# Four convolution layers on 4 x 384 x 64 x 64: the last layer's first input loaded during the mixer, its stores issued by GpSimd, its maxima taken by pieces, and layer 1's taps handed over per band

## The chip, the cores and the metric

The kernel runs on one core of a Trainium2 chip. The core has a matrix engine (TensorE, PE in the profile; PEld is its weight load), VectorE (DVE), ScalarE (ACT), GpSimd (POOL) and SyncE (SP, which only issues DMAs). Every engine works through its own list of instructions in order and waits on semaphores; a DMA that an engine issues also has its place in that list. The metric is the device time of one execution in microseconds; less is better. Everything is float32.

## The reference

The input is 4 batches of 384 channels by 64 x 64 points. Four layers follow one another, each added to its input: `x = x + layer(_gn(x))`, where `_gn` normalizes each batch over 32 groups of 12 channels.

- Layer 0: attention over the 4096 points on the first 96 channels, then a 384 x 384 projection of all channels.
- Layer 1: a 384 x 384 product, a filter in the Fourier domain of each 8 x 8 tile, a depthwise 3 x 3 convolution (nine taps per channel), `gelu(x1) * x2` of the two halves of the channels, and a 192 to 384 product.
- Layer 2: depthwise 3 x 3 and 5 x 5 convolutions joined by gates to a "token" map, batch norms over all batches, and a mixer: 384 to 768, GELU, 768 to 384, batch norm. The result is gated against the layer's input.
- Layer 3, per batch and channel, cut to what matters here:

```python
x_avg = x.mean(axis=(2, 3)); x_max = x.max(axis=(2, 3))
x_w  = gelu(x_avg @ w_avg.T + b_avg + x_max @ w_max.T + b_max)
xr   = (x_w[:, :, None] * w_mix[None, :, :]).reshape(b, c, 7, 7)
Gx   = sqrt(sum(xr * xr, axis=(2, 3)));  Nx = Gx / (Gx.mean(axis=1) + EPS)
kern = gamma * (xr * Nx) + beta
out  = depthwise 7x7 convolution of x with kern, one kernel per batch and channel
```

The layer sees `_gn(x)`, so the 7 x 7 kernels of a batch are known only when that batch's mean, variance and maximum per channel are known, over all three groups of 128 channels. And layer 2's last batch norm needs the mixer's output of all four batches before any batch of layer 3 can start.

## The kernel before, in words

The 384 channels are three groups `j` of 128 partitions. The Python program emits instructions batch by batch; a scheduler then sets the order on each engine, with the place in the program as its priority, and pools of buffers decide when a tile's memory comes free for the next.

**Layers 0 and 1** (`phase_a`, 0 to about 2426 us). Attention of batch b is emitted side by side with layer 1 of batch b − 1 (`layer1`, L787 to L823). Layer 1 goes by tiles of 8 rows and 16 columns: `h` counts the eight bands of 8 rows, `w` the four tiles in a band. When a band and its neighbours are there, `band_taps` (L897 to L930) makes the depthwise convolution: for each channel group nine taps, nearly all on VectorE (L918), then the GELU and the product of the halves. It is a generator: with each `next` it hands over one channel group, at the tiles w = 1, 2, 3 of a later band. `band_out` (L932 to L942) makes the last product and stores. In the last batch (`alone`), where no attention runs beside it, some taps go to TensorE instead.

**Layer 2** (`phase_b`, then `phase_ef`, L1274). After the convolutions come two loops. The first (E, 3250 to 3764 us) makes the 384 to 768 product and stores it (`hidden`, stored from ACT's queue, L1372). It also makes `wx`, the part of the result that does not pass the mixer, and stores it from GpSimd's queue (L1371). The second (F, the mixer, 3772 to 4268 us) loads blocks of `hidden` of 128 x 6 x 1024 (L1385, 3 MB each), applies the GELU (L1387), multiplies (L1397), copies out (L1404), takes statistics (L1405), and stores `h2` in blocks of 128 x 3 x 1024 from GpSimd's queue (L1407). The last batch's `h2` stays on the chip (`h2_last`). The pools of E and F are opened together and closed together.

**Layer 3** (`phase_g`, L1428) takes the batches in the order 3, 0, 1, 2.

- `x2_of(b)` (L1555 to L1625) makes the input of layer 3 for a batch: for j = 1, 2, 0 it loads `wx` (2 MB, L1564, SP), and for each of four pieces of 1024 columns loads `h2` (L1570, not for batch 3), scales it on ACT into PSUM (L1574), adds it into x on VectorE (L1575) and squares on ACT with a running sum (L1577). Then VectorE takes the maximum over all 4096 columns in one instruction (L1579). For j = 1 and 2, x is stored for later (L1584, SP). After the third group come the small steps of the norm (L362 to L380), the two small products for `x_w` (L1595), its GELU (L1605) and the scales `a_s`, `a_b`, `b_s` (L1608 to L1621).
- The dense part of the 7 x 7 kernel is made from `w_mix` and a band matrix as Toeplitz tiles and run on TensorE; `to_strips` (L1627) scales x and transposes it into `z` for that. The constant part (`beta`) is a 7 x 7 box sum, made by `boxes` (L1692 to L1761): sums of rows on GpSimd (L1725, L1727) and VectorE, a transpose and a product with `cols7` on TensorE (L1748, L1754), added into x (L1756); the finished x of a batch and channel group is stored as `rest` (L1760, SP; the DRAM side has 4096 runs of 512 bytes).
- `phase_g` emits `x2_of(b)` step by step with `to_strips` and `boxes` for j = 0 of the batch before. When all four batches are through, `conv7` (L1657 to L1690) runs over j = 0, 1, 2: GpSimd makes each third Toeplitz tile and VectorE the others (L1668), TensorE multiplies (L1681), VectorE adds `rest` (L1689). Beside it `half_strips` (L1508) and `boxes` prepare j = 1 and 2; those load the stored x2.
- The x tiles are 16 KB per partition; three buffers with the tag `x` serve `x2_of` and the later boxes. A tile of j = 1, 2 is free when its store has landed, that of j = 0 only when the boxes are through and the `rest` store has landed.

Of the kernel before, what the change touches and what calls it, by code (L numbers as in the profile page):

```python
# [28 lines left out]
NJ = 3  # L29
P = 128  # L30
# [196 lines left out]
class _Builder:  # L227
# [550 lines left out]
    def layer1(self, b):  # L778

        nc = self.nc
        st = self.stats_tile("x1_st")
        norm, alone = self.norm1, b == B - 1
        if alone:
            self.tap_weights()
        xb, tt, cf, acc = {}, {}, {}, {}  # L787
        for n in range(-2, 4 * 11):
            h, w = n // 4, n % 4
            if n + 2 < 32:  # L790
                if (n + 2) % 4 == 0:
                    x = self.block("xa_in", self.xa[b], (n + 2) // 4, bufs=1)
                xb[n + 2] = self.tile_norm(x, (n + 2) % 4, norm, alone)
            if n < 0:
                continue
            if n < 32:
                tt[n] = self.tile_hidden(xb.pop(n))
            if 0 < n < 33:
                cf[n - 1] = self.tile_filter(tt.pop(n - 1))
            if 1 < n < 34:  # L800
                self.tile_back(cf.pop(n - 2), (n - 2) // 4, (n - 2) % 4)
            if n < 34:
                yield 3.75

            if w == 1 and 0 < h < 9:
                self.halo(h - 1)
            if w == 1 and 1 < h < 10:
                acc[h - 2] = []
                taps = self.band_taps(h - 2, alone, acc[h - 2])
            if w and 1 < h < 10:  # L810
                next(taps, None)
                yield 0.0
            if w == 0 and h > 2:
                k = h - 3
                yield from self.band_out(b, acc.pop(k), k, st)
        r, gm, n, mv = self.norm_of_stats(st)
        nc.vector.tensor_copy(self.r2[:, :, b], r)
        nc.vector.tensor_copy(self.n2[:, :, b], n)
        nc.vector.tensor_sub(self.p2[:, :, b], mv[:, :, 0], gm)
        nc.vector.tensor_mul(self.p2[:, :, b], self.p2[:, :, b], r)  # L820
# [450 lines left out]
        nc.vector.scalar_tensor_tensor(self.about, self.c1_u, -1.0, self.base, ALU.mult, ALU.subtract)  # L1271
        yield

    def phase_ef(self):  # L1274
        tc, nc = self.tc, self.nc
        with ExitStack() as ctx:
            self.open_psum(ctx)
            cp = ctx.enter_context(tc.tile_pool(name="e_const", bufs=1))
            io = ctx.enter_context(tc.tile_pool(name="e_io", bufs=2))
            hp = ctx.enter_context(tc.tile_pool(name="e_h", bufs=2))  # L1280
            w1 = self.weight(cp, "cm_w1_t")
            w2 = self.weight(cp, "cm_w2_t")
            cg1 = self.weight(cp, "cg_w1_t")
            cg2 = self.weight(cp, "cg_w2_t")

            a, c = self.bn_scale_shift("bn_ar", *self.over_batches("ar", self.mvt), self.vec("ar_g"), self.vec("ar_b"))
            gp = self.sm([P, NJ, B], "gp")
# [31 lines left out]
                nc.vector.tensor_mul(self.gn[:, j, :], self.n2[:, j, :], stay)  # L1319


            st = cp.tile([P, 6, B * 8, 6], F32, tag="h_st", name="h_st")
            sums = cp.tile([P, NJ, B, 4], F32, tag="wx_sum", name="wx_sum")
            for b in range(B):
                for i in range(4):
# [50 lines left out]
            a1, c1 = self.bn_scale_shift("bn_h", mv[:, :, 0], mv[:, :, 1], self.vec("cm_g1"), self.vec("cm_b1"))  # L1376


            st2 = cp.tile([P, NJ, B * 8, 6], F32, tag="h2_st", name="h2_st")
            mvb = cp.tile([P, NJ, B, 2], F32, tag="h2_mvb", name="h2_mvb")  # L1380
            for b in range(B):
                for i in range(4):
                    blk = slice(i * 1024, (i + 1) * 1024)
                    h = hp.tile([P, 6, 1024], F32, tag="h", name="f_h")
                    nc.sync.dma_start(h, self.hidden[b][:, :, blk].rearrange("o p n -> p o n"))  # L1385
                    for o in range(6):
                        nc.scalar.activation(  # L1387
                            h[:, o, :], h[:, o, :], AF.Gelu, bias=c1[:, o : o + 1], scale=a1[:, o : o + 1]
                        )
                    out = self.h2_last[:, :, blk]  # L1390
                    if b < B - 1:
                        out = io.tile([P, NJ, 1024], F32, tag="x", name="f_h2")
                    for j in range(NJ):
                        for v in range(2):
                            m = self.pm("h2_m")
                            for o in range(6):
                                nc.tensor.matmul(  # L1397
                                    m,
                                    lhsT=w2[:, o, j * P : (j + 1) * P],
                                    rhs=h[:, o, v * 512 : (v + 1) * 512],  # L1400
                                    start=o == 0,
                                    stop=o == 5,
                                )
                            nc.scalar.copy(out[:, j, v * 512 : (v + 1) * 512], m)  # L1404
                            nc.vector.bn_stats(st2[:, j, 8 * b + 2 * i + v, :], out[:, j, v * 512 : (v + 1) * 512])  # L1405
                    if b < B - 1:
                        nc.gpsimd.dma_start(self.h2[b][:, :, blk], out)  # L1407
                for j in range(NJ):
                    nc.vector.bn_aggr(mvb[:, j, b], st2[:, j, 8 * b : 8 * b + 8].rearrange("p a b -> p (a b)"))
            mv = self.sm([P, NJ, 2], "h2_mv")  # L1410
# [18 lines left out]
    def phase_g(self):  # L1429
# [8 lines left out]
        with ExitStack() as ctx:  # L1438
            self.open_psum(ctx, 3)
            cp = ctx.enter_context(tc.tile_pool(name="g_const", bufs=1))  # L1440
            self.gx_p = ctx.enter_context(tc.tile_pool(name="g_x", bufs=1))
            self.gw_p = ctx.enter_context(tc.tile_pool(name="g_w", bufs=2))
            self.gt_p = ctx.enter_context(tc.tile_pool(name="g_t", bufs=2))
            self.w_gate = []
# [63 lines left out]
    def half_strips(self, j, half):  # L1508

        nc = self.nc  # L1510
        for pair in range(2):
            for part in range(3):
                y = self.gx_p.tile([P, 11 * P], F32, tag="y", name="ax2", bufs=2)
                lo, hi = (22 * part - 1) * W, (22 * part + 21) * W
                inside = slice(max(lo, 0) - lo, min(hi, N) - lo)
                for u in range(2):
# [38 lines left out]
    def x2_of(self, b):  # L1555
# [2 lines left out]
        nc = self.nc  # L1558
        mv = self.sm([P, NJ, 2], "gn_mv")
        mx = self.sm([P, NJ], "max")  # L1560
        for j in (1, 2, 0):
            at = lambda v: v[:, j, b : b + 1]
            x = self.gx_tile("x2")
            nc.sync.dma_start(x, self.wx[b][:, j])  # L1564
            var = self.sm([P, 4], "x2_var")
            for q in range(4):
                sl = slice(q * 1024, (q + 1) * 1024)
                if b < B - 1:
# [6 lines left out]
                nc.vector.tensor_add(x[:, sl], x[:, sl], m)  # L1575

                nc.scalar.activation(h, x[:, sl], AF.Square, bias=at(self.neg2), accum_out=var[:, q : q + 1])  # L1577
                yield None
            nc.vector.tensor_reduce(mx[:, j : j + 1], x, AX.X, ALU.max)  # L1579
            nc.vector.tensor_copy(mv[:, j, 0:1], at(self.mean2))  # L1580
            nc.vector.tensor_reduce(mv[:, j, 1:2], var, AX.X, ALU.add)
            nc.vector.tensor_scalar(mv[:, j, 1:2], mv[:, j, 1:2], 1.0 / N, None, ALU.mult)
            if j:
                nc.sync.dma_start(self.scratch["x2"][b][j], x)  # L1584
        r, gm, n, _ = self.norm_of_groups(mv, True)
        avg = self.sm([P, NJ], "avg")
        nc.vector.tensor_sub(avg, mv[:, :, 0], gm)
# [38 lines left out]
    def to_strips(self, j, b, x):  # L1626
# [1 line left out]
        nc = self.nc  # L1628

        for part in range(3):  # L1630
            y = self.gx_p.tile([P, 11 * P], F32, tag="y", name="ax2", bufs=2)
            lo, hi = (22 * part - 1) * W, (22 * part + 21) * W
            if part == 0:
                nc.gpsimd.memset(y[:, 0:W], 0.0)
# [57 lines left out]
    def boxes(self, j, b, x):  # L1692
# [8 lines left out]
        for part in range(4):  # L1701
# [55 lines left out]
                if q == 0:  # L1757
                    yield
            if part == 3:
                nc.sync.dma_start(self.rest[j][:, :, b], x.rearrange("p (y n) -> p y n", n=P))  # L1760
            yield  # L1761


# [1 line left out]
def tile_conv_preact4(ctx, tc, ins, out):  # L1765
    k = _Builder(ctx, tc, ins, out)
    with ExitStack() as strips:
        k.phase_a(strips)
        k.phase_b()
        k.phase_ef()  # L1770
        k.phase_g()
    return k

# [17 lines left out]
```

## Time and profile before

| | |
|---|---|
| runs before | 5096.59, 5099.97, 5101.0 us; median 5099.97 us |
| profiled execution: its own time | 5109.2 us |
| its span | 5107.4 us |
| mean granted clock of TensorE | 0.947 |
| busy in the span: PE, PEld | 4618.5 us (90%), 2618.1 us (51%) |
| busy: DVE, ACT, POOL | 2736.5 us (54%), 2080.9 us (41%), 730.1 us (14%) |
| last matmul of the mixer ends | 4268.3 us |
| scales of batches 3, 0, 1, 2 ready (L1620) | 4352.7, 4406.9, 4501.7, 4577.4 us |
| dense convolution starts (L1681) | 4591.3 us |

The profiled execution is one of its own and was 9 us longer than the median of the runs. Times in the text are counted from the start of its span. "Busy" is the time in which an engine worked on something; a wait names the instruction whose end released the waiting one. A group of rows "x12" has twelve instructions, and its mean is that of one.

### The profile page before, as it was taken

The page shows a single profiled execution, that of the slowest core. Times are in us where ns is not written, and L with a number is a line of the kernel's source. Part 1 is how long each engine was busy: PE and PEld are TensorE (multiplying, and loading weights), DVE is VectorE, ACT ScalarE, POOL GpSimd, SP SyncE. Part 2 cuts the span into 40 slices and gives each one's busy share as a digit, 9 for nine tenths or more (in the row PEclk, how much of TensorE's full clock was granted, in tenths as well). Part 3 has the DMA queues.
Part 4 walks back from the last instruction along what each step waited for, and adds up shares of the span by engine and source line. Part 5 has one row for each costly group of instructions (what it writes and reads, how often), then busy time and mean ns, then how long its engine had stood idle before and what let it go on. Part 6 is the DMA issues. An engine that isn't in the chain of part 4 may idle for free. (4 is left out here: it accounts for less than half of the span.)

```text
span 5107.4 us, 47835 instructions
## 1 busy us (share of the span) xinstructions
PE 4618.5 (90%) x17875; PEld 2618.1 (51%) x17875; DVE 2736.5 (54%) x4432; ACT 2080.9 (41%) x2789; POOL 730.1 (14%) x524
## 2 busy tenths in 40 slices
PE   5999999989999999999988999599999995559999
PEld 2333444334443344435467888244444442448999
DVE  5322566634556445555867877554421114658775
ACT  4444344454444544445345665311133334652320
POOL 1000000000000000000035555000000000125433
PEclk9999999999999999998989999799999997569999
DMA  5210211111112101112259999766644434658776
GB/s 171 62 48 29 89 62 62 56 50 44 56 62 77 38 31 62 62 60 91 90 165 274 293 294 286 248 245 241 231 181 148 152 149 166 241 165 247 219 225 189
DMA packets 387541, 723.28 MB, mean 142 GB/s; under 512 B 21627, under 2 KB 221158, under 8 KB 380390
## 3 DMA queue, kind: packets, MB, share of 16 engines
q1 hardware_dynamic: 333528, 519.50, 32.8%
q10 hardware_dynamic: 28494, 105.99, 5.3%
q0 software_dynamic: 25280, 94.65, 4.8%
q8 instruction: 144, 2.36, 0.2%
q14 instruction: 95, 0.78, 0.0%
HBM read 432.48 MB, written 287.57 MB: 141 GB/s over the span
## 5 line engine op out<-in xcount | busy, mean ns | idle before, releaser
L733 PE MATMUL av<-probs,vt 128*128 128x512 f32 x2048 | 972.3, 612 | 0.0
L704 ACT ACTIVATE probs<-sc_s 128x1024 f32<-128x1024 f32 x512 | 498.4, 1020 | 784.1 <-PE av L733 767.6
L733 PEld LDWEIGHTS av<-probs,vt 128*128 128x128 f32 x2048 | 377.9, 195 | 482.6 <-issue 478.9
L1127 PE MATMUL conv_m<-toep,z 128*128 128x256 f32 x2304 | 521.6, 386 | 11.1 <-DVE toep L1108 6.8
L918 DVE SCALAR_TENSOR_TENSOR acc<-band,vecs,acc 128x512 f32<-128x512 f32 x708 | 507.3, 747 | 45.0 <-POOL band L879 24.0
L1397 PE MATMUL h_m<-f_h,cm_w_t 128*128 128x512 f32 x1152 | 496.2, 594 | 7.9 <-ACT f_h L1387 7.9
L1127 PEld LDWEIGHTS conv_m<-toep,z 128*128 128x128 f32 x2304 | 440.3, 193 | 72.9 <-DVE z L1060 4.9
L1348 PE MATMUL h_s<-e_tok,cm_w_t 128*128 128x512 f32 x768 | 364.5, 598 | 5.4 <-DVE e_tok L1333 5.4
L1681 PE MATMUL conv_m<-toep,z 128*128 128x128 f32 x3072 | 364.3, 277 | 1.2 <-DVE rest_o L1689 1.1
L1397 PEld LDWEIGHTS h_m<-f_h,cm_w_t 128*128 128x128 f32 x1152 | 219.4, 191 | 284.7 <-issue 273.9
L1108 POOL TENSOR_TENSOR toep<-w,band 128x1536 f32<-128x1536 f32 x94 | 323.5, 3442 | 285.9 <-PE conv_m L1127 248.1
L1681 PEld LDWEIGHTS conv_m<-toep,z 128*128 128x128 f32 x3072 | 355.3, 194 | 1.6 <-issue 1.3
L696 PE MATMUL sc_s<-q,k 32*128 32x512 f32 x2048 | 301.9, 647 | 13.0 <-ACT probs L704 10.3
L841 PE MATMUL t_m<-w_in_t,xb 128*128 128x384 f32 x768 | 277.1, 495 | 1.8 <-DVE coef L858 0.9
L766 PE MATMUL proj_m<-xm,w_proj_t 128*128 128x512 f32 x576 | 268.0, 604 | 7.3 <-DVE xm L719 7.3
L1355 ACT COPY e_h<-h_s 128x1024 f32<-128x1024 f32 x96 | 97.2, 1012 | 419.1 <-PE h_s L1348 419.1
L773 DVE SCALAR_TENSOR_TENSOR x_res<-proj_m,bn_c,x_res 128x512 f32<-128x512 f32 x96 | 71.8, 748 | 348.7 <-PE proj_m L766 345.7
L1348 PEld LDWEIGHTS h_s<-e_tok,cm_w_t 128*128 128x128 f32 x768 | 147.7, 192 | 192.3 <-issue 185.6
L1357 DVE BATCH_NORM_STATS2 h_st<-e_h 128x6 f32<-128x512 f32 x192 | 123.4, 685 | 188.7 <-ACT e_h L1355 188.6
L1405 DVE BATCH_NORM_STATS2 h_st<-f_h 128x6 f32<-128x512 f32 x72 | 50.0, 694 | 322.8 <-ACT f_h L1404 322.8
L841 PEld LDWEIGHTS t_m<-w_in_t,xb 128*128 128x128 f32 x768 | 142.1, 191 | 139.2 <-issue 61.7
L1348 PE MATMUL h_s<-z,cm_w_t 128*128 128x512 f32 x384 | 198.7, 600 | 12.5 <-DVE z L1333 12.5
(365 smaller groups left out, 6216.4 us busy)
## 6 DMA issues: line engine op xcount, KB each, us to landing
d<-d_o ACTq DMA_DIRECT2D x96, 512.0 KB
c_d<-d SPq DMA_DIRECT2D x96, 512.0 KB
hid<-e_h ACTq DMA_DIRECT2D x16, 3072.0 KB
f_h<-hid SPq DMA_DIRECT2D x16, 3072.0 KB
x_in<-in_x SPq DMA_DIRECT2D x96, 256.0 KB
x_res<-in_x SPq DMA_DIRECT2D x32, 768.0 KB
xa<-x_res POOLq DMA_DIRECT2D x32, 768.0 KB, 3.9
xa_in<-xa SPq DMA_DIRECT2D x32, 768.0 KB
```

Of the source, the lines that this page charges most:

```text
L696: nc.tensor.matmul(s[:, g], lhsT=k4[32 * g : 32 * g + 32, c], rhs=q[i][32 * g : 32 * g + 32], start=True, stop=True,)
L704: nc.scalar.activation(p[:, h * 1024 : (h + 1) * 1024], s[:, 2 * h : 2 * h + 2].rearrange("p a b -> p (a b)"), AF.Exp, scale=0.25,)
L733: nc.tensor.matmul(av, lhsT=vt[:, 4 * c + v, :], rhs=p[:, v * 512 : (v + 1) * 512], start=c == 0 and v == 0, stop=c == 7 and v == 3,)
L766: nc.tensor.matmul(m, lhsT=self.w_proj[:, j, o * P : (o + 1) * P], rhs=xm[:, j], start=j == 0, stop=j == NJ - 1,)
L841: nc.tensor.matmul(m[:, 0:C], lhsT=xb[:, j], rhs=self.w_in[:, j, :], start=j == 0, stop=j == NJ - 1,)
L918: nc.vector.scalar_tensor_tensor(out, src(j, k), w, done, ALU.mult, ALU.add)
L1108: eng.tensor_tensor(t, self.w53[:, at : at + 192].rearrange("p (m n) -> p m n", n=8).unsqueeze(2).to_broadcast([P, 24, 8, 8]), band.rearra ...
L1127: nc.tensor.matmul(m[:, c * 256 : (c + 1) * 256], lhsT=self.z_[:, at : at + P], rhs=t[:, 12 * c + 4 * i : 12 * c + 4 * i + 4].rearrange("p ...
L1348: nc.tensor.matmul(s[:, v, :], lhsT=w1[:, j, o * P : (o + 1) * P], rhs=t[j][:, v * 512 : (v + 1) * 512], start=j == 0, stop=j == NJ - 1,)
L1357: nc.vector.bn_stats(st[:, o, 8 * b + 2 * i + v, :], h[:, o, v * 512 : (v + 1) * 512])
L1397: nc.tensor.matmul(m, lhsT=w2[:, o, j * P : (j + 1) * P], rhs=h[:, o, v * 512 : (v + 1) * 512], start=o == 0, stop=o == 5,)
L1681: nc.tensor.matmul(m[:, ch * P : (ch + 1) * P], lhsT=self.z_[:, at : at + P], rhs=t[:, 8 * c + 2 * i : 8 * c + 2 * i + 2].rearrange("p m a ...
```

## The change

Five edits, in the order of the diff.

1. In `layer1`, for the first three batches, all three channel groups of a band's taps are emitted at once at tile w = 1, those of bands 6 and 7 together. In the last batch they are emitted group by group as before.
2. `phase_ef` closes E's pools (`e_const`, `e_io`) before F. In the memory that is released, on the right side, the pool of the x tiles is opened already there, with batch 3's three tiles (`x2_ahead`). Their loads from `wx` are emitted in the mixer's last batch, one at each of the blocks i = 1, 2, 3. F's output tiles are 128 x 1024, three of them, and `h2` is stored in 36 pieces instead of 12. The strips' tiles (`ax2`) move to another pool.
3. `x2_of` takes batch 3's tiles from that list and loads the others as before.
4. Its maximum is taken by pieces of 1024 columns, each behind its piece's square, and a last instruction takes the maximum of the four.
5. The stores of x2 and of `rest` are issued by GpSimd instead of SP.

```diff
-            if w == 1 and 1 < h < 10:
+            if alone and w == 1 and 1 < h < 10:
                 acc[h - 2] = []
                 taps = self.band_taps(h - 2, alone, acc[h - 2])
-            if w and 1 < h < 10:
+            if alone and w and 1 < h < 10:
                 next(taps, None)
+                yield 0.0
+            if not alone and w == 1 and 1 < h < 9:
+                for k in (6, 7) if h == 8 else (h - 2,):
+                    acc[k] = []
+                    for _ in self.band_taps(k, alone, acc[k]):
+                        pass
                 yield 0.0
...
+    x2_order = 1, 2, 0
+
-    def phase_ef(self):
+    def phase_ef(self, strips):
...
+            cp = ctx.enter_context(tc.tile_pool(name="ef_const", bufs=1))
             w2 = self.weight(cp, "cm_w2_t")
+            hp = ctx.enter_context(tc.tile_pool(name="ef_h", bufs=2))
+            first = ctx.enter_context(ExitStack())
+            ep = first.enter_context(tc.tile_pool(name="e_const", bufs=1))
+            io = first.enter_context(tc.tile_pool(name="e_io", bufs=2))
...
+            first.close()
+            self.gx_p = strips.enter_context(tc.tile_pool(name="g_x", bufs=1, side="right"))
+            self.x2_ahead = [self.gx_tile("x2") for _ in range(NJ)]
+            io = ctx.enter_context(tc.tile_pool(name="f_io", bufs=3))
...
-                    out = self.h2_last[:, :, blk]
-                    if b < B - 1:
-                        out = io.tile([P, NJ, 1024], F32, tag="x", name="f_h2")
+                    if b == B - 1 and 0 < i:
+                        j = self.x2_order[i - 1]
+                        nc.sync.dma_start(self.x2_ahead[i - 1], self.wx[b][:, j])
                     for j in range(NJ):
+                        out = self.h2_last[:, j, blk]
+                        if b < B - 1:
+                            out = io.tile([P, 1024], F32, tag="x", name="f_h2")
...
-                    if b < B - 1:
-                        nc.gpsimd.dma_start(self.h2[b][:, :, blk], out)
+                        if b < B - 1:
+                            nc.gpsimd.dma_start(self.h2[b][:, j, blk], out)
...
-            x = self.gx_tile("x2")
-            nc.sync.dma_start(x, self.wx[b][:, j])
-            var = self.sm([P, 4], "x2_var")
+            if b == B - 1:
+                x = self.x2_ahead.pop(0)
+            else:
+                x = self.gx_tile("x2")
+                nc.sync.dma_start(x, self.wx[b][:, j])
+            var, top = self.sm([P, 4], "x2_var"), self.sm([P, 4], "x2_max")
...
                 nc.scalar.activation(h, x[:, sl], AF.Square, bias=at(self.neg2), accum_out=var[:, q : q + 1])
+                nc.vector.tensor_reduce(top[:, q : q + 1], x[:, sl], AX.X, ALU.max)
                 yield None
-            nc.vector.tensor_reduce(mx[:, j : j + 1], x, AX.X, ALU.max)
+            nc.vector.tensor_reduce(mx[:, j : j + 1], top, AX.X, ALU.max)
...
             if j:
-                nc.sync.dma_start(self.scratch["x2"][b][j], x)
+                nc.gpsimd.dma_start(self.scratch["x2"][b][j], x)
...
             if part == 3:
-                nc.sync.dma_start(self.rest[j][:, :, b], x.rearrange("p (y n) -> p y n", n=P))
+                nc.gpsimd.dma_start(self.rest[j][:, :, b], x.rearrange("p (y n) -> p y n", n=P))
```

In the order of instructions that the scheduler makes of the changed program, the three loads of batch 3's x do not stand in the mixer's last batch: they stand on SP directly behind the load of the mixer's first `hidden` block and ahead of the second, and wait for the end of E. On GpSimd the `x2` and `rest` stores stand among the box sums of the next batch and, in the convolution, among the Toeplitz tiles.

## The prediction

> **What bounds the kernel now.** I read the slices first, then stage windows, then the order of time across the seam between mixer and last layer, then the waits of the last layer, then the rows of GpSimd's own DMA issues. The slices:
>
> ```profile
> PE   5999999989999999999988999599999995559999
> PEclk9999999999999999998989999799999997569999
> ```
>
> TensorE is the bound nearly everywhere; four slices are half empty, and three of them lie together near the end, where its clock drops too. The windows of the mixer, of what lies between it and the dense 7x7 convolution (I call it the head), and of that convolution (columns: stretch, length, busy of PE, PEld, DVE, ACT, POOL, clock, DMA share, GB/s):
>
> ```profile
> 3772.00:4268.30 496.30, 496.21 (x1152) 219.39 (x1152) 71.81 (x108) 161.75 (x191) 8.62 (x12) 1.00 0.36 135
> 4268.30:4591.30 323.00, 145.81 (x706) 130.43 (x705) 199.50 (x318) 192.30 (x270) 54.62 (x53) 0.58 0.61 219
> 4591.30:5107.40 516.10, 487.51 (x4196) 479.81 (x4196) 370.64 (x413) 120.70 (x206) 230.10 (x139) 0.98 0.75 220
> ```
>
> The mixer leaves PE no gap, and a third of the DMA is used: room for loads. In the head no engine is busy over 62%: a chain of dependences sets it. There the change has its place. The seam in order of time (start, length, instruction):
>
> ```profile
> 4273.92 1.21 ACT L1574 ACTIVATE x_m<-z,g,gh 128x1024 f32<-128x1024 f32 x1 [1.11 <-DVE g L1420]
> ...
> 4276.55 2.12 SPq L1564 DMA_DIRECT2D x<-wx  x3
> ...
> 4286.91 2.35 DVE L1575 TENSOR_TENSOR x<-x,x_m 128x1024 f32<-128x1024 f32 x2 [7.57 <-DMA x<-wx]
> ...
> 4293.84 1.19 ACT L1574 ACTIVATE x_m<-z,g,gh 128x1024 f32<-128x1024 f32 x1
> 4294.05 0.32 SPq L1584 DMA_DIRECT2D x<-x  x1
> 4294.06 4.42 DVE L1579 TENSOR_REDUCE max<-x 128x1 f32<-128x4096 f32 x1
> ...
> 4324.70 0.15 DVE L375 TENSOR_TENSOR gn_d<-gn_d,gn_mv 128x3 f32<-128x3 f32 x1
> ```
>
> The scaled h2 piece is there at 4275.13; the add waits for its x until 4286.91. Each channel group then ends in a reduce of 4.42 us. Three groups take 4286.91 to 4321.65, and batch 3's norm starts at 4324.70. Who waits in 4268 to 4592:
>
> ```profile
> POOL box L1725 <- DVE x L1575: 115.6, 6, 37.5
> PE gn_pv L362 <- DVE gn_d L375: 96.4, 4, 46.4
> ```
>
> TensorE waits in all four batches for statistics that end such a row of adds. In the convolution stage, the waits of POOL and PE and of SP's rest stores:
>
> ```profile
> POOL toep L1668 <- PE conv_m L1681: 141.6, 49, 7.6
> ...
> PE box_m L1754 <- ACT ht L1750: 11.4, 7, 4.5
> PE ht_m L1748 <- ACT z L1535: 10.5, 5, 3.8
> ```
> ```profile
> SPq L1760 <- DVE in_x L1756: 21.2, 8, 5.8
> ```
>
> PE loses about 23 us there, so little can be won; POOL makes each third Toeplitz tile, with 2.9 us to spare on average (141.6/49). GpSimd's DMA issues, the nearest rows to the moved stores:
>
> ```profile
> L776 POOL DMA_DIRECT2D xa<-x_res x32 | 23.1, 723 | 648.2 <-DVE x_res L773 648.2
> ...
> L637 POOL DMA_DIRECT2D shift<-zero x16 | 8.7, 554 | 0.9 <-DMA shift<-zero 0.7
> L1407 POOL DMA_DIRECT2D h<-f_h x12 | 8.6, 718 | 419.6 <-ACT f_h L1404 419.6
> ```
>
> **The change part by part.** The sum is made against the profiled execution (span 5107.4, its own time 5109.2); the median of the runs, 5099.97, is 9.2 lower, 0.18%. I take the difference off the median. About 0.2%, 10 us, is what can be told from no change.
>
> *1, batch 3's x2 loads in the mixer.* Three loads leave the seam, so the first add can follow the first scaled piece: 4286.91 − 4275.13 = **11.8 us won**. The price is at the mixer's start. In the new order the three loads (6.3 MB) stand on SP directly behind the first hidden load and ahead of the second, and their memory comes free with the last matmul of the stage before (3764.2). In the old trace the second hidden load landed at 3784.75, its Gelus ended at 3790.5, and PE needs them only after the first block (3772.09 + 30.9 = 3803.0): 12.5 us to spare. 6.3 MB at the 295 to 308 GB/s of the windows there is 21 us late; at the 400 GB/s that a full DMA share would give (135 GB/s at share 0.36 scales to 375; 308 at 0.75 to 410) 16 us late. Loss 3 to 8 us if all three go ahead whole, 0 if the queues share. I take **+3**; ends 0 and +16, if the room is not there at all.
>
> *2, maxima by pieces.* 12 reduces of 4.42 us become 48 of 128x1024 and 12 of 128x4. A piece lies between 1.10 (a quarter of 4.42) and 1.22 (the add of that shape, L1575); 128x4 is 0.15 (L1581). DVE's own work grows by 12 × (4 × 1.16 + 0.15 − 4.42) = 4 us. But the reduces now lie between adds, where DVE waited for ACT: ACT's pair of scale and square takes 2.27 us per piece (4291.58 to 4293.84), DVE's pair 1.22 + 1.16 = 2.4. A group becomes 4 × 2.4 + 0.45 small = 10.1 against 11.58. Three groups: **4.4 us won**. Further on in the chain of batch 3 one more 4.42 reduce, of the next batch, stood before the gate's row (L1608) at 4341.4: **4.4 won**. With part 1, batch 3's scales (4352.7 in the old trace) come 20 us earlier. Batches 0, 1, 2 have the same tail, 4.42 ahead of their statistics; their adds have bubbles anyway, so I take half of 3 × 3.3: **5 won**; ends 0 and 20 (both reduces out of each chain).
>
> *3, does the 20 us survive.* Batch 1's second group waits for the x tile that batch 3's box filter held: rest store at 4416.51, load behind it at 4417.73 to 4422.6, while scales of batches 0, 1, 2 stood at 4406.9, 4501.7, 4577.4 and the convolution started at 4591.3. The box filter starts from batch 3's scales, so it moves with them, and with it each later link. I carry all 20; ends 5 (the later batches are set by DVE and ACT, 199.5 and 192.3 of 323 us busy) and 35 (SP's loads no longer stand behind stores that wait: the x stores held SP 54.6 + 8.1 us, the rest stores 50.8 in the head).
>
> *4, stores by GpSimd.* 8 x2 stores of 128 rows of 16 KB: 0.54 (128 rows, shift) to 0.72 (384 rows, xa, h2), hidden, as POOL is 17% busy in the head. The 12 rest stores write 4096 runs of 512 B, which no row of POOL shows. Flat: 0.72. From the two rows, 540 ns at 128 and 721 at 384 give 0.71 ns a run, so 0.45 + 2.9 = 3.3 us. In proportion to 384 rows: 7.7 us. I take 3.3, since both ends of that line are measured. Behind each stand box adds and Toeplitz tiles, and the store first waits for the last box add (2.65 us on SP on average, 21.2/8). With 2.9 us of slack and four Toeplitz buffers I take 0.5 us of PE for each of the 8 in the convolution: **+4**; ends −2 and +45 (8 × (7.7 + 2.65 − 4.7) at the proportional price). SP, free of waiting, loads the next strips earlier: ACT waited 64.8 us for them, PE only 10.5 behind it: **−2**, ends −10 and 0.
>
> The Trainium skill, "DMA: Bandwidth & Descriptors", speaks both ways here: by "SWDGE vs HWDGE vs iDMA" GpSimd's descriptors are computed by software and SP's by hardware, with faster setup, while "Anatomy of one DMA" says of descriptor generation "You can emit a lot of descriptors before the incremental cost shows up". By the second sentence a rest store would stay near the flat row and the sum would be 4 us better; by the first it could be any of the prices above, and no row here decides.
>
> *5, h2 stores in 36 pieces.* 36 × 0.54 to 0.72 on POOL, idle in the mixer (8.6 of 496 us): nothing; what hides it is PE's unbroken 496 us, and the last store must land before batch 0's first h2 load, 124 us after the third batch's end: nothing.
>
> *6, taps of layer 1.* For three batches a band's taps are handed over at once. The instruction order of VectorE hardly changes: the taps stand in 224 groups with other work between them, against 210 before. PE waits for their sums in this stage 23 us in all (out_m on acc, 14.8 + 8.6). I take **0**; ends −12 and +25 (one 0.75 us tap ahead of PE's next operand in each of 32 bands).
>
> Sum: −11.8 − 4.4 − 4.4 − 5 + 3 + 4 − 2 = −20.6, so **5079 us**.
>
> **The rivals.** *Only the first batch gains* (0.14): the x tiles and DVE set batches 0 to 2, 5 of 20 us arrive, nothing of the other 5: −5 + 3 + 4 − 2 = 5100, and about 5090 with half of both. For: both engines at 60% in the head. Against: PE's four waits for gn_d.
>
> *GpSimd's stores hold the Toeplitz tiles* (0.16), the one on the other side: a rest store costs POOL the proportional 7.7 us and more. PE uses a POOL tile each 3 × 8 × 0.277 = 6.6 us, POOL needs 2.35 for it and about 1.3 for box adds; past some 5 us a store, wait included, PE stops. 45 us lost less the 25 won: 5120 to 5145. For: 4096 runs, and POOL 45% busy there. Against: the small slope between 128 and 384 rows.
>
> *Taps in lumps delay PE* (0.09): +25 on −21: 5104, up to 5120. Against: the order.
>
> *The head tightens as a whole* (0.11): SP's unblocked loads and both reduces of each chain: −20 − 20 − 15 + 5 = 5050, down to 5040.
>
> **How the numbers follow.** My forecast has 0.50, with its own range 5062 to 5092. Faster by over 0.2%: 0.48 of it, 0.11 of the tight head, 0.05 of the first rival, 0.64. Within: 0.02 + 0.08 + 0.03 = 0.13. Slower: 0.16 + 0.06 + 0.01 = 0.23. The range, 5045 to 5130, leaves out the lower half of the tight head and the upper half of GpSimd's case, and some of sums of them.
>
> **What would show it.** Right: the first add within 2 us of the first scaled piece; gn_d of batch 3 some 16 us sooner after the last mixer matmul; the head some 300 us long instead of 323; PE unbroken in the mixer; POOL's rest stores near 3 us. Wrong: rest stores at 7 us or more with PE waiting for POOL's Toeplitz tiles; a head still near 320 us; a gap of PE after the mixer's first block; a longer layer-1 stage.

## The result and the profile after

The changed kernel takes 5033.18 us (median; 5018.58 to 5036.5 in its runs) against 5100.38 us (5096.59 to 5101.0): ratio 0.9864, 95% interval 0.9844 to 0.9885. That is 67 us faster, outside my range (5045 to 5130) and three times the 21 us that I forecast. Its profiled execution took 5036.04 us, with a span of 5034.1. The two spans differ by 73.3 us, more than the medians, as the profiled execution before was 9 us slower than its kernel's median and the one after 3 us.

To see where the time went I cut both profiled executions at the same points: the end of attention's last matmul (end of stage A), the first matmul of loop E, the last matmul of the mixer, and the first dense 7x7 matmul.

| us | before | after | change |
|---|---|---|---|
| stage A (0 to the last attention matmul) | 2293.3 | 2262.6 | −30.7 |
| rest of layer 1, layer 2's convolutions | 898.0 | 894.4 | −3.6 |
| gap to the first matmul of E | 58.3 | 50.4 | −7.9 |
| E, and the 7.9 us to the mixer | 522.5 | 518.8 | −3.7 |
| mixer | 496.2 | 496.2 | 0 |
| head | 323.0 | 291.8 | −31.2 |
| convolution stage | 516.1 | 519.9 | +3.8 |

I had put 25.6 us on the head, +3 on the mixer and +2 on the convolution, and nothing on the first four. The 3.6 us of the second row and the 3.7 of the fourth are no more than all the kernels of this document differ by there (891.8 to 902.5 us, and 518.8 to 523.6). The slices of the changed kernel's page and the windows of its mixer, head and convolution stage (columns as in the prediction):

```profile
PE   5999999989999899999989999699999996569999
PEclk9999999999999999998989999799999997569999
```
```profile
3725.00:4222.40 497.40, 496.18 (x1152) 219.39 (x1152) 71.61 (x108) 163.66 (x191) 19.14 (x36) 1.00 0.39 147
4222.40:4514.20 291.80, 149.49 (x730) 135.47 (x730) 200.22 (x371) 193.30 (x272) 62.80 (x65) 0.59 0.63 225
4514.20:5034.10 519.90, 486.44 (x4174) 479.65 (x4172) 370.77 (x409) 118.88 (x203) 244.67 (x148) 0.97 0.73 217
```

PE has lost none of its mixer, the head is as busy as before in microseconds but shorter, and the convolution stage is a little emptier. The seam, in order of time, beside the lines that the prediction showed:

```profile
4228.03 1.21 ACT L1593 ACTIVATE x_m<-z,g,gh 128x1024 f32<-128x1024 f32 x1 [1.11 <-DVE g L1437]
...
4229.51 1.22 DVE L1594 TENSOR_TENSOR x<-x,x_m 128x1024 f32<-128x1024 f32 x1
...
4231.88 0.44 ACTq L1464 DMA_DIRECT2D w_gate<-in_w_max_t  x1
4232.35 1.28 ACT L1477 ACT_TABLE_LOAD   x1 [3.12 <-DVE x_max L1597]
...
4234.89 2.32 ACT L1593 ACTIVATE x_m<-z,g,gh 128x1024 f32<-128x1024 f32 x2
4236.11 1.22 DVE L1594 TENSOR_TENSOR x<-x,x_m 128x1024 f32<-128x1024 f32 x1 [2.61 <-ACT x_m L1593]
```

The first add now stands 7.1 us after the last mixer matmul instead of 18.6: 11.5 us won, as forecast (11.8). But the second stands at 13.7: ACT first issues six loads of the gate's weights (L1464, on its own queue) and takes the root of the summed `w_mix`. That wait had lain behind the DMA and was not in my sum.

### The profile page after: what moved, and what is told of

Same layout as the page of the kernel before. It is cut to its first block, busy times and chain, and to the rows that moved or that the text cites. A ratio compares the mean times of both kernels' runs of the same rounds, so it can differ in the third digit from the quotient of the medians.

```text
span 5034.1 us, 48007 instructions
## 1 busy us (share of the span) xinstructions
PE 4606.5 (92%) x17875; PEld 2617.1 (52%) x17875; DVE 2735.1 (54%) x4480; ACT 2119.4 (42%) x2819; POOL 762.6 (15%) x568
## 5 line engine op out<-in xcount | busy, mean ns | idle before, releaser
L1414 PE MATMUL h_m<-f_h,cm_w_t 128*128 128x512 f32 x1152 | 496.2, 594 | 7.9 <-ACT f_h L1401 7.9
```

The lines of the kernel that those rows point to most:

```text
L1414: nc.tensor.matmul(m, lhsT=w2[:, o, j * P : (j + 1) * P], rhs=h[:, o, v * 512 : (v + 1) * 512], start=o == 0, stop=o == 5,)
```

## What happened in stage A

The waits of PE from 128 us to the end of layer 1 (2426 us before, 2400 after), first of the kernel before, then of the changed one (total, times, longest):

```profile
PE back_m L866 <- ACT t_t L849: 26.3, 15, 2.4
PE ln_v L590 <- ACT ln_rs L588: 15.6, 8, 4.1
PE out_m L936 <- DVE acc L926: 14.8, 4, 8.6
```
```profile
PE out_m L942 <- DVE acc L932: 15.2, 4, 9.1
...
PE back_m L872 <- ACT t_t L855: 8.0, 7, 1.5
```

The waits for the taps' sums (`out_m` on `acc`), which I had watched, did not move. One that I had not looked at did: `back_m` for `t_t`, ACT's copy of the tile product out of PSUM. Up to the end of stage A itself it fell from 24.3 to 6.1 us. ACT in order of time at the end of one band, and PE's wait, before:

```profile
656.04 1.28 ACT L922 ACT_TABLE_LOAD   x1
657.34 0.63 ACT L922 ACTIVATE acc<-acc 128x512 f32<-128x512 f32 x1
660.30 0.63 ACT L925 ACTIVATE acc<-acc 64x512 f32<-64x512 f32 x1 [2.34 <-DVE acc L918]
661.69 0.72 ACT L916 ACTIVATE acc<-band,vecs 128x512 f32<-128x512 f32 x1 [0.76 <-DVE acc L926]
662.32 0.46 ACT L849 COPY t_t<-t_m 128x384 f32<-128x384 f32 x1
...
662.83 0.94 PE L866 MATMUL back_m<-to_pos,coef 128*128 128x128 f32 x6 [2.36 <-ACT t_t L849]
```

and after:

```profile
656.89 0.63 ACT L928 ACTIVATE acc<-acc 128x512 f32<-128x512 f32 x1
657.53 1.28 ACT L704 ACT_TABLE_LOAD   x1
658.83 1.02 ACT L704 ACTIVATE probs<-sc_s 128x1024 f32<-128x1024 f32 x1
659.75 0.47 ACT L855 COPY t_t<-t_m 128x384 f32<-128x384 f32 x1
660.24 1.28 ACT L931 ACT_TABLE_LOAD   x1
661.53 0.63 ACT L931 ACTIVATE acc<-acc 64x512 f32<-64x512 f32 x1
```

Before, ACT does a band's first GELU, then stands 2.34 us in its order for VectorE to end the taps of the second, does that, waits again, and only then copies `t_t`; PE, whose `back_m` waits for that copy, stood from 660.5 to 662.8. After, the scheduler lets ACT go back to the softmax's exponentials and the copy between the two GELUs. It costs more table loads (236 in the trace against 206), on an engine that is busy for 42% of the span.

## The experiments

Each table gives the profiled execution's stage A, gap before E, head and convolution stage in us, then the median and the ratio with its interval. The kernel before had 2293.3, 58.3, 323.0 and 516.1 in its profile, and a median of 5102.4 beside the first group of runs, 5106.9 beside the second, 5099.4 beside the third, and 5102.3 and 5102.8 beside the first four and the last two of the fourth.

**One edit alone.** Each is the kernel before with one part of the change; for the second, the diff is all of `phase_ef` and the x tiles' pool, with maxima and stores as before.

| | A | gap | head | conv. | median | ratio |
|---|---|---|---|---|---|---|
| taps_alone | 2264.1 | 55.8 | 317.1 | 519.9 | 5071.78 | 0.9942 (0.9925 to 0.9958) |
| ahead_alone | 2290.1 | 51.6 | 317.1 | 514.8 | 5089.08 | 0.998 (0.9964 to 0.9996) |
| maxima_alone | 2290.0 | 56.7 | 303.1 | 515.5 | 5086.12 | 0.997 (0.996 to 0.9981) |
| stores_alone | 2288.2 | 57.1 | 301.7 | 523.5 | 5094.05 | 0.9986 (0.9976 to 0.9996) |

taps_alone:

> Only the first edit: layer 1's taps of batches 0 to 2 handed over per band. Theory: in the profile after, ACT goes back to the softmax's exponentials and the copy of t_t between a band's two GELUs, where before it stood still 2.3 us behind the first GELU for the second one's input; PE's waits of back_m for t_t fall from 26 to about 7 us and the stage ends 25 to 31 us sooner, so the time is 5070 to 5076 us. Rival, the stage's 30 us come from the run (the granted clock, other memory) and not from this edit: 5095 to 5105. My prediction's own step (nothing): 5100.

ahead_alone:

> Only the second edit: E's pools closed before the mixer, batch 3's three x loads ahead, h2 stored in 36 pieces. Theory: the first add of the last layer follows the first scaled piece, 11 to 12 us won at the seam; and the gate's weights, which now lie in other memory, are loaded some 60 us earlier, so E starts some 8 us sooner after the convolutions: 5080 to 5084 us. Rival, the 8 us before E belong to the taps' edit or to the run: 5088 to 5092. Rival, the seam's 12 us are lost again further on because the x tiles and VectorE set the later batches: 5092 to 5100.

maxima_alone:

> Only the maxima by pieces. By the prediction's step 4 to 9 us in batch 3's chain and 5 in the others: 5088 to 5092 us. Rival, VectorE's 4 us more work and the busy engines of the head eat it: 5098 to 5104.

stores_alone:

> Only the stores of x2 and rest issued by GpSimd. The profile after shows 1.66 us of GpSimd for a rest store and 0.55 for an x2 store. Theory: SP no longer stands before these stores and loads sooner, which the head gets back: 5 to 12 us faster, 5088 to 5095. Rival, GpSimd's waits in front of the stores hold box sums and Toeplitz tiles: 5102 to 5115. The prediction's step (4 lost, 2 won): 5102.

Up to the head the stages come apart cleanly. Stage A falls by 29 us with the taps' edit alone and by 3 to 5 with the others, which leave its code as it was; the gap falls by 7 with the pools; the convolution stage grows with the stores. In the head three edits win 6, 20 and 21 us alone, and 31 together. Part of that is not theirs: the link from batch 0's scales to batch 1's took 94.8 us in the profile before, and 88.6 in taps_alone, whose head is the same code. The whole head of that same code took 323.0, 317.1, 316.4, 316.8 and 324.2 us in the five kernels that have it (the kernel before, taps_alone and three that follow). So ahead_alone's 6 us can't be told from nothing, the maxima alone win 13 to 21 us, the stores alone 15 to 23, and all together 25 to 33. Of the medians the four edits alone win 31, 13, 16 and 8 us, some 69 in all, against 67 for the whole change.

**What belongs to which part.** without_taps is the changed kernel with `layer1` as before. pools_alone is ahead_alone without its loads:

```diff
-            self.x2_ahead = [self.gx_tile("x2") for _ in range(NJ)]
...
-                    if b == B - 1 and 0 < i:
-                        j = self.x2_order[i - 1]
-                        nc.sync.dma_start(self.x2_ahead[i - 1], self.wx[b][:, j])
...
-            if b == B - 1:
-                x = self.x2_ahead.pop(0)
-            else:
-                x = self.gx_tile("x2")
-                nc.sync.dma_start(x, self.wx[b][:, j])
+            x = self.gx_tile("x2")
+            nc.sync.dma_start(x, self.wx[b][:, j])
```

tt_by_vector is the kernel before with one copy moved, rest_by_sync the changed kernel with one store moved back:

```diff
-        nc.scalar.copy(tt, m[:, 0:C])
+        (nc.scalar.copy if alone else nc.vector.tensor_copy)(tt, m[:, 0:C])
...
-                nc.gpsimd.dma_start(self.rest[j][:, :, b], x.rearrange("p (y n) -> p y n", n=P))
+                nc.sync.dma_start(self.rest[j][:, :, b], x.rearrange("p (y n) -> p y n", n=P))
```

| | A | gap | head | conv. | median | ratio |
|---|---|---|---|---|---|---|
| without_taps | 2291.2 | 50.2 | 291.8 | 522.1 | 5068.69 | 0.9924 (0.9907 to 0.994) |
| pools_alone | 2293.7 | 50.4 | 310.0 | 510.0 | 5080.04 | 0.9951 (0.9934 to 0.9968) |
| tt_by_vector | 2313.1 | 57.3 | 316.4 | 515.9 | 5128.57 | 1.0045 (1.0029 to 1.0062) |
| rest_by_sync | 2263.5 | 50.0 | 297.7 | 514.5 | 5039.65 | 0.9867 (0.9851 to 0.9884) |

without_taps:

> The changed kernel with layer 1's taps as before. Theory, the edits add up: the 30 us that the taps' edit gave alone come back, 5060 to 5067 us, and stage A ends where it did before, at about 2293 us of the span. Rival, the edits share a gain (an earlier clock, shifted transfers): 5040 to 5050.

pools_alone:

> The second edit without its loads ahead: E's pools closed early, h2 stored in 36 pieces, but batch 3's x loaded where it was. Theory: E starts some 8 us sooner, because the gate's weights are loaded while the convolutions before still run, and the seam waits for x as before: 5092 to 5096 us. Rival, the loads ahead give all of that edit's gain: 5100 to 5104. Rival, the pools give all of it: 5086 to 5091.

tt_by_vector:

> The kernel before, with the copy of t_t in batches 0 to 2 made by VectorE instead of ACT, and nothing else. Theory: PE waited for t_t because the copy stood on ACT behind a GELU that waits for VectorE's taps; off ACT it no longer does, the waits of back_m for t_t go from 26 to under 10 us and the stage ends 10 to 25 us sooner: 5077 to 5092 us. Rival: VectorE's rows of up to nine taps of 0.75 us delay the copy as much: 5100 to 5115.

rest_by_sync:

> The changed kernel with the rest stores issued by SP again; the x2 stores stay with GpSimd. Theory: the convolution stage gets back the 4 us that it lost (520 against 516 us), since GpSimd no longer waits for the last box sum ahead of its Toeplitz tiles, and the head loses some of its gain as SP's loads stand behind stores: 5030 to 5042 us. Rival, the rest stores are what the stores' edit gave (some 7 us): 5040 to 5048. Rival, they cost: 5022 to 5029.

without_taps gives stage A back to within 2 us: the edits add up. pools_alone won more than any theory of mine said, and shows why the name of the second edit misleads. SyncE in pools_alone, where the loads are emitted in the last layer:

```profile
3729.75 0.39 SPq L1392 DMA_DIRECT2D f_h<-hid  x1
3749.02 1.29 SPq L1570 DMA_DIRECT2D x<-wx  x3
```

They are issued 505 us before the mixer's end, as in the changed kernel and in ahead_alone. (ahead_alone, with the same seam, has a head 7 us and a convolution stage 5 us longer than pools_alone; what makes that difference stays open.) What holds a load is the memory of its tile; once the pool opens at E's end, the scheduler puts the load there, wherever it is emitted. The gap before E goes with the pools too. Before, ACT stood in its order behind the issue of the gate's weights of E, ahead of a batch norm's root:

```profile
3223.45 8.73 ACTq L282 DMA_DIRECT2D cg_w_t<-in_cg_w_t  x2
3232.21 1.28 ACT L312 ACT_TABLE_LOAD   x1 [11.64 <-DMA cm_w_t<-in_cm_w_t]
```

In the changed kernel these two loads are issued at 3163.83 and 3165.78, 7 us behind the convolutions' last matmul (32 us before) and 25 ahead of that root, and hold nothing.

tt_by_vector was meant to take the wait away and moved it instead. Its waits of PE in stage A begin with:

```profile
PE back_m L866 <- DVE t_t L849: 45.6, 28, 4.9
```

The copy now stands behind rows of taps on VectorE: the rival had the cause, though 5129 us lies beyond its 5100 to 5115. It does show that the copy is what PE waits for: the wait grew by 21 us and the stage by 20. rest_by_sync gives the convolution stage 5 us back and takes 6 from the head: no gain.

**The cause in stage A, and the emission.** gelu_after_tt is the kernel before, taps spread as before, in which a band's second GELU takes as its bias a zero made of the tile's `t_t`, so that it can't be put ahead of that copy:

```diff
             if w and 1 < h < 10:
+                self.tt_now = tt.get(n)
                 next(taps, None)
...
+                none = 0.0
+                if not alone and self.tt_now is not None:
+                    none = self.sm([P, 1], "none")
+                    nc.gpsimd.tensor_scalar(none, self.tt_now[:, 0:1], 0.0, None, ALU.mult)
+                    none = none[0:64]
-                nc.scalar.activation(acc[0][64:P], acc[2][0:64], AF.Gelu)
+                nc.scalar.activation(acc[0][64:P], acc[2][0:64], AF.Gelu, bias=none)
```

taps_own_place is the kernel before with a band's taps at once and bands 6 and 7 not joined:

```diff
-            if w == 1 and 1 < h < 10:
+            if alone and w == 1 and 1 < h < 10:
                 acc[h - 2] = []
                 taps = self.band_taps(h - 2, alone, acc[h - 2])
-            if w and 1 < h < 10:
+            if alone and w and 1 < h < 10:
                 next(taps, None)
                 yield 0.0
+            if not alone and w == 1 and 1 < h < 10:
+                acc[h - 2] = []
+                for _ in self.band_taps(h - 2, alone, acc[h - 2]):
+                    pass
+                yield 0.0
```
loads_in_place makes the diff of pools_alone in the changed kernel. seam_free belongs to the next group, whose edits it holds.

| | A | gap | head | conv. | median | ratio |
|---|---|---|---|---|---|---|
| gelu_after_tt | 2252.2 | 58.2 | 316.8 | 516.7 | 5060.97 | 0.9929 (0.9901 to 0.9957) |
| taps_own_place | 2266.4 | 57.2 | 324.2 | 515.2 | 5076.38 | 0.9958 (0.9944 to 0.9972) |
| loads_in_place | 2260.2 | 50.9 | 291.8 | 523.1 | 5040.13 | 0.9887 (0.9856 to 0.9918) |
| seam_free | 2266.8 | 51.1 | 283.1 | 516.6 | 5033.35 | 0.9872 (0.9842 to 0.9901) |

gelu_after_tt:

> The kernel before, its taps spread as before; only the second GELU of a band takes its bias from a zero made of the tile's t_t, so that it can't stand on ACT ahead of that copy. Theory: the place of the t_t copy behind two GELUs was the whole cause of the stage's 30 us; with the copy between them the waits of back_m for t_t fall under 8 us and the stage ends 18 to 30 us sooner, 5072 to 5085 us. Rival, the taps' own time on VectorE or the order on PE matters more: waits of back_m as before or moved to out_m, 5092 to 5110.

taps_own_place:

> The kernel before, with a band's taps handed over at once but bands 6 and 7 each at its own time. Theory, the handing over at once counts: 25 to 31 us sooner, 5070 to 5078 us, as with bands 6 and 7 together. Rival, the last two bands together give it: 5095 to 5103.

loads_in_place:

> The changed kernel, but batch 3's loads emitted in the last layer, where they were. Theory: closing E's pools early is what lets the scheduler put the loads at the mixer's start, wherever they are emitted; the loads are issued there as before and the time is that of the changed kernel, 5028 to 5042 us. Rival, the emission counts: 11 us slower, 5042 to 5053.

seam_free:

> The changed kernel with the root of w_mix early, the rest stores of the second and third group by SP, and the six loads of the gate's weights of the last layer issued by GpSimd instead of ACT, which issues them for 3.5 us between the first and second scaled piece. Theory: the second piece follows 2 us behind the first instead of 5.7 to 6.9, the head gets 4 us back: 5015 to 5025 us. Rival, batch 3 no longer sets the end: as the kernel with the first two edits, 5021 to 5030.

gelu_after_tt decides it. With the taps spread as before and only that one GELU held back, stage A ends 41 us sooner than before, more than the 18 to 30 of its theory, and sooner than in the changed kernel by 10. PE's wait for the copy (to 2400 us; 2.9 of it in stage A), and the windows of stage A before, after and in gelu_after_tt:

```profile
PE back_m L867 <- ACT t_t L850: 4.8, 7, 1.0
```
```profile
0.00:2293.30 2293.30, 2149.53 (x7058) 931.13 (x7059) 1146.59 (x1923) 1004.15 (x1215) 88.90 (x181) 0.98 0.19 62
0.00:2262.60 2262.60, 2139.15 (x7060) 927.32 (x7061) 1146.00 (x1924) 1041.95 (x1244) 87.96 (x181) 0.98 0.18 63
0.00:2252.20 2252.20, 2136.63 (x7058) 928.25 (x7059) 1149.33 (x1923) 1052.60 (x1251) 94.90 (x199) 0.98 0.19 63
```

The wait itself is 18 of the 31 us in the changed kernel and 21 of the 41 here. PE's busy time for the same matmuls fell too, by 10 and 13 us. The traces show TensorE at half clock for 89 us of stage A before, 75 after and 68 here (85 to 102 in the six kernels with the stage's code as before, 58 to 82 in the thirteen with the taps handed over at once or the GELU held back), and a matmul of `av` took 1.06 us at half clock against 0.59. By these figures I estimate that 6 and 9 us of the shorter busy time come from the clock; no run tests that, and the rest, smaller waits among it, stays open.

So the order of ACT, not the handing over of taps as such, was worth the time; handing them over at once happened to give the better order in most bands (taps_own_place: nearly the same without joining bands 6 and 7). loads_in_place has the changed kernel's stages throughout: the emission of the loads in the mixer is worth nothing once the pool is open.

**A faster version.** rest_split leaves only the rest stores of the first channel group, which fall into the head, with GpSimd; mix_early takes the root of the summed `w_mix` ahead of the mixer; "both" has both; seam_free, above, adds that GpSimd issues the six gate loads. after_again is the changed kernel beside them.

```diff
-                nc.gpsimd.dma_start(self.rest[j][:, :, b], x.rearrange("p (y n) -> p y n", n=P))
+                (nc.sync if j else nc.gpsimd).dma_start(self.rest[j][:, :, b], x.rearrange("p (y n) -> p y n", n=P))
```
```diff
+            sq = self.sm([P, NJ, 49], "mix_sq", 1)
+            nc.vector.tensor_mul(sq.rearrange("p j k -> p (j k)"), self.vec("w_mix"), self.vec("w_mix"))
+            self.mix2 = strips.enter_context(tc.tile_pool(name="g_mix", bufs=1, side="right")).tile(
+                [P, NJ], F32, tag="mix2", name="mix2"
+            )
+            nc.vector.tensor_reduce(self.mix2, sq, AX.X, ALU.add)
+            nc.scalar.activation(self.mix2, self.mix2, AF.Sqrt)
             st2 = cp.tile([P, NJ, B * 8, 6], F32, tag="h2_st", name="h2_st")
...
-                    nc.scalar.dma_start(t[:, i], self.ins[k][:, j])
+                    nc.gpsimd.dma_start(t[:, i], self.ins[k][:, j])
```

The last two lines are seam_free's alone.

| | A | gap | head | conv. | median | ratio |
|---|---|---|---|---|---|---|
| after_again | 2261.2 | 50.8 | 291.4 | 522.0 | 5039.89 | 0.9878 (0.9861 to 0.9894) |
| rest_split | 2259.4 | 49.9 | 285.2 | 509.7 | 5021.38 | 0.9848 (0.9827 to 0.987) |
| mix_early | 2260.2 | 51.1 | 280.6 | 519.9 | 5025.71 | 0.9851 (0.9836 to 0.9866) |
| both | 2257.6 | 50.9 | 290.5 | 509.4 | 5024.83 | 0.9848 (0.9831 to 0.9866) |
| tt_split | 2250.9 | 51.1 | 284.8 | 516.6 | 5013.76 | 0.9824 (0.981 to 0.9837) |
| tt_split_mix | 2256.7 | 50.0 | 281.1 | 505.8 | 5011.76 | 0.9822 (0.9808 to 0.9836) |

after_again:

> The changed kernel once more, beside the three that follow, as their measure on the same chip: 5025 to 5045 us, 1.3 to 1.5% under the kernel before.

rest_split:

> The changed kernel, with the rest stores of the second and third channel group, which fall into the convolution stage, issued by SP again; those of the first group, in the head, stay with GpSimd. Theory: the head keeps its 292 us and the convolution stage falls from 520 to about 515, as with all of them on SP: 4 to 6 us under the changed kernel. Rival, it is the last batch's store of the head that makes the stage longer (18.5 us from the last scales to the convolution, 14 otherwise): no change within 2 us.

mix_early:

> The changed kernel, with the square root of the summed w_mix taken before the mixer instead of at the seam. In the trace after, ACT waits at the seam for that sum and loads a table for the root, so the second scaled piece starts 6.9 us behind the first. Theory: this wait ate 4 to 5 of the 11.5 us that the x tiles won; without it batch 3's scales come 4 to 5 us sooner and the time is 4 to 5 us under the changed kernel. Rival, batch 3 is not what the later links wait for any more: no change within 2 us.

both:

> Both of these edits: if each holds, 8 to 11 us under the changed kernel; else as the one that holds.

tt_split:

> The changed kernel with two edits: layer 1's taps spread as before but the second GELU held behind the copy of t_t, and the rest stores of the second and third group issued by SP. If the stages add up: the first stage ends at 2252 us of the span as with that GELU alone, 10 us sooner than in the changed kernel, the convolution stage is 10 us shorter: 5013 to 5022 us against 5033 to 5040.

tt_split_mix:

> The same with the root of w_mix taken before the mixer. If the earlier second piece counts, 2 to 10 us less than without it; in the two kernels that had it so far the head took 281 and 291 us against 285 without, so no change within 5 us is as likely.

rest_split won more than I expected, 12 us in the convolution stage and 6 in the head. With the same stores the convolution stage took 509.4 and 505.8 us in "both" and tt_split_mix, but 516.6 in seam_free and tt_split, so some 5 of the 12 came in each. Its convolution stage:

```profile
4507.50:5017.20 509.70, 485.00 (x4174) 477.68 (x4172) 367.51 (x409) 119.23 (x203) 232.43 (x140) 0.98 0.75 221
```

mix_early moved batch 3's scales by only 2 us (65.9 us after the mixer against 67.8), yet those of the other batches came 10 to 15 us sooner; in "both" they came 1 to 6 us sooner. seam_free brought the second scaled piece to 1.1 us behind the first and, against "both", batch 3's scales 4 us and the convolution's start 7 us forward; its convolution stage was 7 us longer and its time no better. In the head, then, a small shift changes what follows in the later batches by as much as the shift is worth; which of these gains is the edit's own stays open. tt_split (rest_split's store, the taps of before with gelu_after_tt's GELU) keeps the first stage's gain inside the changed kernel. With tt_split_mix it is the fastest here, some 90 us under the kernel before, and the intervals of both ratios (up to 0.9837 and 0.9836) lie below those of the changed kernel (from 0.9844, and from 0.9861 in after_again). Between these two there is no difference.

## Why the prediction was wrong, and where it was right

*What bounds the kernel.* The head was the right place for what I put there. Wrong was to take stage A, where PE is 94% busy, for one without anything to win: 24 us of it were one wait, in the list of waits, and I read only the wait of `out_m` there.

*Part 1, loads ahead.* "So the first add can follow the first scaled piece: 11.8 us won" came out as 11.5 us (shown); what failed is what follows it, 4 of them lost to ACT's gate loads and root (pools_alone: norm of batch 3 at 49.4 us after the mixer instead of 56.4, so 7.0 kept; the second add, at 13.7 us in the changed kernel, stood at 12.5 with the root moved, and at 8.0 in seam_free with the loads moved too). The price of +3 was 0. The second hidden load did come 14 us later against the mixer's start (26.8 us behind it instead of 12.7), near the forecast 16, but PE takes the six slices of a block one after the other and ran on: their last GELU ended at 3760.4, some 3 us after PE had begun the block. (The 12.5 us to spare were counted to 3790.5, the end of the fifth of six GELUs; the sixth ended at 3792.1.) Missing was the gap before E: the same pools let E's gate weights load 25 us earlier against the convolutions' last matmul, 7 to 8 us won. And the mechanism's name was wrong: the pool does it, not the emission.

*Part 2, maxima.* The size of a piece's reduce, "between 1.10 and 1.22", was 1.21 (x48). The whole was forecast at 13.8 us for all four batches; alone it gave 16 us of the median and 13 to 21 of the head. Batch 3's scales came 9.7 us sooner, forecast 8.8.

*Part 3, does it survive.* Batch 3's scales came 16.5 us sooner (84.3 to 67.8 after the mixer) instead of 20, batch 0's only 6.7, batch 1's 28.7, the convolution 31.2. "I carry all 20" was near for the sum by luck, and wrong for each link: batch 0's link grew (54.3 to 64.1, and to 65.0 with the maxima alone), batch 1's shrank (94.8 to 72.8).

*Part 4, stores by GpSimd.* The rows of POOL in the changed kernel:

```profile
L1780 POOL DMA_DIRECT2D rest<-in_x x8 | 13.2, 1655 | 5.2 <-PE conv_m L1701 5.2
L1780 POOL DMA_DIRECT2D rest<-x x4 | 6.7, 1670 | 12.2 <-DVE x L1776 8.7 <-issue 2.2 <-DVE box L1748 1.3
L1604 POOL DMA_DIRECT2D x<-x x8 | 4.4, 554 | 63.7 <-DVE x L1594 55.7 <-DVE xw L1624 5.9 <-DVE gx_n L1636 2.0
```

A rest store costs GpSimd 1.66 us, half of the 3.3 that I drew through two rows, so the sign-turning rival (7.7 and more) fell. The convolution stage lost 3.8 us, forecast +2; the spread over all kernels with and without the later rest stores on GpSimd, 520 to 523.5 against 506 to 520, puts it nearer 8 (means of 521.8 and 514.1). The head's gain from the stores alone, 15 to 23 us, was in no term of the sum; it stood only in the upper end of part 3 and in the rival of the head that tightens as a whole.

*Part 5* held. *Part 6, taps:* "The instruction order of VectorE hardly changes … I take 0; ends −12 and +25" is the step that failed: the term taken as 0 measured −30.7, beyond its end of −12. I compared the order of VectorE alone; the order that counted was ACT's, which makes 30 more table loads in the trace. In its place the runs showed that PE waited for a copy on ACT behind a GELU that waited for VectorE (26.3 us in 15 waits, 8.0 in 7 after). With the 8 us of the gap, which had no term either, this is most of what the forecast missed. The end of −12 was put together from the wait that I knew, not from the largest wait of that stage.

## What to carry to other kernels

When a change alters when work is handed to a scheduler, compare the order on every engine and start from the waits of the engine that bounds the stage, however small a share they are: here a wait of 24 us, 1% of the stage, led to 31 us of the gain. An instruction that waits in order on a helper engine holds all behind it, so look for the short copy that frees a PSUM buffer behind a function that waits for another engine. And ask of a prefetch what holds the load: if it is the memory, opening the pool is the edit and the place of the call is not.

## What the runs showed of the hardware

A DMA issued by GpSimd took it 0.53 us with 128 runs (the h2 pieces), 0.72 with 384 and 1.66 with 4096 of 512 bytes: about 0.28 ns for each further run from end to end ((1.66 − 0.53) / 3968), but 0.7 between 128 and 384, which is why the line through these two gave twice the truth. The result agrees with the Trainium skill, "DMA: Bandwidth & Descriptors", "Anatomy of one DMA", that many descriptors can be emitted before the cost shows, and the runs say how much shows: 1.13 us more for 4096 runs than for 128. Switching ACT between its functions 30 times more often, at 1.28 us each (38 us of ACT's time), came with a stage A that is 31 us shorter.
